# A perceiver block's delta rule: hand-laid order for TensorE and ScalarE, a quartered load of the coefficients, and a last round that also carries the MLP's gate weights and first u

## The chip, the cores and the metric

The kernel runs on one core of a Trainium2 chip. Its time is the device time of one launch, in microseconds (us), taken as the median of several runs. Before the change the median of 3 runs is 2965.88 us (2964.45 to 2977.48). All arithmetic of the parts told of here is in float32.

## What is computed

The input x has 128 sequences of 32 tokens and 512 features, 4096 tokens in all. Three layers follow each other, each with a layer norm ahead and its input added behind: a cross attention to a context, the layer shown here, and a feed-forward part with Hadamard rotations and ternary weights. The middle layer is the one that the change touches:

```python
h = _rms(x, attn_norm_w)
q = silu(silu(_causal_dwconv(h @ Wq.T, conv_q)))   # k and v likewise, with their weights
q = _l2norm(q.reshape(B, T, nh, hd))               # k likewise: each head divided by its length
beta = jax.nn.sigmoid(h @ Wbeta.T)
# for each token t in order, with a 16 x 16 state S for each of 32 heads:
#   err = S k_t - v_t;  S = S - beta_t * err k_t^T;  o_t = S q_t
o = _rms(o, out_norm_w) @ Wout.T
x = x + o
h2 = _rms(x, mlp_norm_w)
x = x + silu(h2 @ Wgate.T) * (h2 @ Wup.T) @ Wdown.T
```

The delta rule over 32 tokens is not run as a scan. Products k k^T and k q^T over the tokens of a sequence are formed first; a triangular substitution then gives a vector u for each token; and o is the masked product of k q^T with u, times 1/|q|.

## The kernel before, in words

The work stands in four stages, one after the other: cross attention (to about 690 us), the delta rule's products (`delta_products`, 696 to 1208 us), the delta rule's output with the MLP (`delta_out_mlp`, 16 blocks of 256 tokens, to about 2400 us), and the Hadamard feed-forward part.

**Rounds of the products.** `delta_products` goes through 8 groups of 512 tokens, a round each (`a_round`). A round has 12 channels of 128 features, four for each of q, k and v, in the order k0 q0 k1 q1 ... v0 v1 v2 v3. For one channel (`channels`), TensorE multiplies normed tokens hT by a slice of the weights into a PSUM bank pp (4 float32 matmuls of 128x512, L568; pp has three banks), ScalarE scales the bank into acc with the last tap of the convolution (L573), and VectorE adds the three other taps (L575). ScalarE then applies the silu twice (`activated`, L582 and L583). Between the channels a round also does this:

- `multiply` takes one *piece* (four heads' worth of products for 256 tokens, function `products`): 32 small matmuls into two banks pg (L495), a copy by ScalarE to kk (L501), a store of the coefficients to the DRAM tensor ld (L502), a masking by GpSimd (L506) and a store to pd (L507). One operand of a piece, kqm, is a copy of k and q laid out with zeros between, filled by eight small loads on SP's queue (`masked_operand`, L481). There are three kqm tiles, and hold fills one as soon as it is free. A round has eight pieces.
- `add` squares k and q on ScalarE (L619) and sums them per head, with beta's product, into the bank pn (L621 to L623). `lengths` takes the roots (tile f). `by_tokens` turns |k| and beta to tokens (L636), and inverts |k| squared and |q|. The latter is a maximum and a reciprocal on 32 partitions x 512 (L648, L649), stored to the DRAM tensor rq (L651).
- `put_v` turns v to tokens (L660), multiplies by |k| into vt (L663), adds beta as a last column (GpSimd, L667) and stores to vd (L669). It is done for the previous round's group in the first four channels of a round. For the last group it follows at the end, after `by_tokens`.
- `normed` prepares the next group's hT: a load, hn on VectorE (L559), four transposes and a copy.

**The substitution beside it.** `Substitution.solve` reads one group's coefficients (tile L, 2 MB, one load, L451 ff.) and vd (tile W). Its 32 steps are on VectorE: a short multiply (L458), a long product pr (L462) and a long subtraction (L468), whose length falls from 31 x 64 elements to 64. Steps are placed beside the rounds and, at a given pace, beside the MLP's blocks (`mixed` takes the next step of whichever list is least far along by its stated costs).

**Order on an engine.** The tile scheduler orders each engine's instructions by the program and its estimates; an engine executes its own list in order, and so does SP with its DMA issues. A class `InOrder` ties every instruction of an engine to the one before it. Before the change only the Hadamard stage uses it.

**The passage to the MLP.** The last round has the products of its own group left over: k and q go to a DRAM tensor kd (SP), and `late_products` does the eight pieces later, from kd, one per MLP block after the first ones. `delta_out_mlp` opens its own SBUF pools: weights wo (1 MB), wg and wu (2.8 MB each, loaded in two parts), wd (2.8 MB). It clears the operand tiles um, pe and km on GpSimd (L759). Then `back(0)` makes the first block's input: a load of u, GpSimd's copy into um (L791), 16 loads into pe per tile (L798), 32 matmuls (L805), oT (L818), a square, and the product with wo (L838), then y, its square, the root, and hT (L853). `load_rows` is L103. wg, wu are scaled by the norm's weights on ScalarE (L929), wo on VectorE. `mlp(b)` computes, for each of 11 slices, gate (L864) and up (L867), then silu and product, and at the end the down product (L875).

In the order of the SP queue before, wd follows `back(0)`'s first u load and stands before the second:

```python
load_rows(nc, wo, woT)
...
for cols in (slice(0, 6 * P), slice(6 * P, FF)):
    for t, src in ((wg, wgT), (wu, wuT)):
        load_rows(nc, t[:, :, cols], src[:, cols])
...
mixed((4.0, part(first, 4.0)), (1.0, part(late, 1.0)))
scaled_rows(nc, st, "onw", onorm_w, [wo])
load_rows(nc, wd, wdT)
```

Of the kernel before, what the change touches and what calls it, by code (L numbers as in the profile page):

```python
# [10 lines left out]
FP = mybir.dt.float32  # L11
# [46 lines left out]
class Ctx:  # L58
# [33 lines left out]
    def transposed(self, ps, x, ident, dtype=FP):  # L92

        rows, n = x.shape[0], x.shape[1] // P
        pt = ps.tile([P, n, rows], dtype, name="ps")
        for c in range(n):
            self.nc.tensor.transpose(pt[:, c, :], x[:, c * P : (c + 1) * P], ident[:rows, :rows])
        return pt


def load_rows(nc, dst, src):

    nc.sync.dma_start(dst, src.rearrange("(c p) n -> p c n", p=P))  # L103
# [15 lines left out]
def butterflies(nc, a, b):  # L119
# [9 lines left out]
    return a  # L129

# [304 lines left out]
class Substitution:  # L435
# [7 lines left out]
    def solve(self, gi):  # L443
        nc = self.nc
        L = self.pool.tile([P, T, H4, T], FP, name="L")
        nc.sync.dma_start(
            L.rearrange("p s h t -> p (s h t)"),
            self.ld[gi].rearrange("c (b s) f -> (c b) (s f)", s=T),
        )
# [7 lines left out]
        for s in range(T):  # L457
            nc.vector.tensor_mul(w[:, s], w[:, s], bc(W[:, s, :, HD], HD))  # L458
# [25 lines left out]
def products(nc, banks, pool, ld, pd, k, m, cm):  # L484
# [4 lines left out]
    for i in range(2):  # L489
        for r, pg in enumerate(pgs):  # L490
            rows = slice(r * P // 2, (r + 1) * P // 2)
            for j in range(4):
                js = slice(j * T, (j + 1) * T)
                ts = slice(i * P + j * T, i * P + (j + 1) * T)
                nc.tensor.matmul(  # L495
# [3 lines left out]
    for r, pg in enumerate(pgs):  # L499
        kk = pool.tile([P, 2, 2, H4, T], FP, name="kk")  # L500
        nc.scalar.copy(kk, pg)  # L501
# [8 lines left out]
        )  # L510


def delta_products(
# [11 lines left out]
    stack, (xp, wp1, hp, wk1, wp, st, wk, wp2, wk2, wp3, wk3, psn, psp, ps, psg) = pools(  # L525
        tc, ("b_x", 3), ("b_w1", 1), ("b_hn", 2), ("b_h", 2), ("b_w", 1), ("b_st", 2), ("b_k", 2),
        ("b_w2", 1), ("b_v", 2), ("b_m", 4), ("b_g", 6), ("b_pn", 1, PSUM), ("b_pp", 3, PSUM),
        ("b_ps", 2, PSUM), ("b_pg", 2, PSUM),
    )
    with stack:  # L530
        w, cw = {}, {}
        for n, src, p in (("k", wkT, wp1), ("q", wqT, wp1), ("v", wvT, wp2)):
            w[n] = p.tile([P, DC, D], FP, name=f"w{n}")
            load_rows(nc, w[n], src)
# [11 lines left out]
        kqm = [wp3.tile([P, H4, 2, KT], FP, name=f"kqm{i}", bufs=1) for i in range(3)]  # L546
# [8 lines left out]
        def normed(n, xt, hT):  # L555
# [6 lines left out]
            nc.scalar.copy(hT[:, :, i * P : (i + 1) * P], g.transposed(ps, hn, g.ident))  # L562

        def channels(hT, n, ec):

            pp = psp.tile([P, GB, T], FP, name="pp")
            for dc in range(DC):
                nc.tensor.matmul(  # L568
# [4 lines left out]
            nc.scalar.activation(acc, pp, AF.Copy, scale=cw[n][:, ec, TAPS - 1 : TAPS])  # L573
# [7 lines left out]
        def activated(acc, dst):  # L581
            nc.scalar.activation(acc, acc, AF.Silu)  # L582
            nc.scalar.activation(dst, acc, AF.Silu)  # L583
# [13 lines left out]
        def multiply():  # L597
# [3 lines left out]
                nc, lambda: psg.tile([P, 2, 2, H4, T], FP, name="pg"), wk3,  # L601
# [6 lines left out]
        class Group:  # L608
# [8 lines left out]
            def add(self, kq, hT, ec):  # L617
                sq = wk.tile([P, 2, SG], FP, name="sq")
                nc.scalar.activation(sq, kq, AF.Square)  # L619
                at = dict(start=ec == 0, stop=ec == DC - 1)  # L620
                nc.tensor.matmul(self.sums[0:H], hs[:, ec, :], sq[:, 0], **at)  # L621
                nc.tensor.matmul(self.sums[H : 2 * H], w["b"][:, ec, :], hT[:, ec, :], **at)
                nc.tensor.matmul(self.sums[2 * H :], hs[:, ec, :], sq[:, 1], **at)  # L623

            def lengths(self):

                f = self.factors = wk.tile([3 * H, SG], FP, name="f", bufs=1)
                nc.scalar.activation(f[H : 2 * H], self.sums[H : 2 * H], AF.Tanh, scale=0.5)
                for r in (slice(0, H), slice(2 * H, 3 * H)):
                    nc.scalar.activation(f[r], self.sums[r], AF.Sqrt)  # L630

            def by_tokens(self):
                f = self.factors
                pt = ps.tile([P, GT, 2 * H], FP, name="ps")
                for i in range(GT):
                    nc.tensor.transpose(  # L636
# [10 lines left out]
                q = f[2 * H :]  # L647
                nc.vector.tensor_scalar_max(q, q, 1e-12)  # L648
                nc.vector.reciprocal(q, q)  # L649
                for c in range(DC):  # L650
                    nc.gpsimd.dma_start(  # L651
                        rq[self.gi, :, :, c].rearrange("i h t -> h i t"),
                        f[2 * H + c * HH : 2 * H + (c + 1) * HH].rearrange("h (i t) -> h i t", t=P),
                    )

            def put_v(self, ec):
                v2 = self.v.pop(ec)
                pv = ps.tile([P, GT, P], FP, name="ps")
                for i in range(GT):
                    nc.tensor.transpose(pv[:, i, :], v2[:, i * P : (i + 1) * P], g.ident)  # L660
# [6 lines left out]
                nc.gpsimd.tensor_copy(vt[:, :, :, HD], self.beta[:, :, h])  # L667
# [5 lines left out]


# [3 lines left out]
        loads = (3, 4, 5, 9)  # L678

        def a_round(gi, old, hT, made):  # L680
# [3 lines left out]
            if gi + 1 < NG:  # L684
                hT_next = wk1.tile([P, DC, SG], FP, name="hT")
                made.append(hT_next)
            for j, (n, ec) in enumerate(todo):
                if n == "v":
                    dst = new.v[ec] = wk2.tile([P, SG], FP, name="v2", bufs=4)
                else:  # L690
                    if n == "k":
                        kq[ec] = wp3.tile([P, 2, SG], FP, name="kq")
# [5 lines left out]

                if due[j] and count["done"] < len(held) and (old or j >= 4):
                    multiply()  # L700
                activated(acc, dst)
                if n == "q":
                    if gi < NG - 1:
                        pieces.extend((gi, ec, half, kq[ec]) for half in range(SG // KT))
                        hold()
                    else:
                        nc.sync.dma_start(kd[:, ec], kq[ec])
                if 3 <= j <= 9 and j % 2:
                    new.add(kq[(j - 3) // 2], hT, (j - 3) // 2)
                if j in loads and gi + 1 < NG:  # L710
                    xt.append(load((gi + 1) * GT + len(xt)))
                if j == 9:
                    new.lengths()
                    if gi == 0:
                        g.factors(*(t[:, EARLY:] for t in stats))
                if j == 11:
                    new.by_tokens()
                if j >= 8 and gi + 1 < NG:
# [678 lines left out]
```

## Time and profile before

| | us |
|---|---|
| median of 3 runs | 2965.88 (2964.45 to 2977.48) |
| the profiled execution | 2972.53 |
| its span | 2970.8 |
| TensorE busy in the span | 2844.7 (96%) |
| VectorE busy | 2006.6 (68%) |
| ScalarE busy | 1042.0 (35%) |
| GpSimd busy | 672.3 (23%) |
| first product of the rounds (k of round 0) | 695.7 |
| starts of rounds 1 to 7 | 756.4, 816.2, 886.0, 956.2, 1019.0, 1088.7, 1156.0 |
| last product of the rounds ends | 1208.2 |
| first gate product of the MLP | 1264.3 |

The profile is of one execution. Its engines are PE (TensorE matmuls), PEld (TensorE's weight loads), DVE (VectorE), ACT (ScalarE), POOL (GpSimd) and SP (DMA issues). A busy time is the time in which an engine executes; L12 is a line of the kernel. The row "PEclk" shows the clock that TensorE was granted, in tenths of full speed. A chain of waits follows the work that ended last back from step to step, each to what released it. Rows of groups give busy time and the mean duration of one in ns, then the idle time ahead of them and what ended it. ScalarE's and VectorE's shares say little here, since the stages differ in what binds them; busy times by stage are more use.

### The profile page before, as it was taken

The numbers are of one execution on the slowest core, as the hardware profiler recorded it, in microseconds if no ns is written. First come the engines' busy times: TensorE is split into PE (matmuls) and PEld (weight loads), VectorE is DVE, ScalarE is ACT, GpSimd is POOL, SyncE is SP. The second block draws the span as 40 slices with busy tenths as digits, with TensorE's granted clock in tenths as the row PEclk, the third lists the DMA queues.
The fourth block names the chain that finished last, engine by engine and source line by source line (L and its number), as shares of the span: only waits on it lengthen the run. The fifth ranks groups of instructions, "written<-read, shape, count | busy, mean of one in ns | idle before, by whom it ended". The sixth has DMA issues, their size and how long they took to land.

```text
span 2970.8 us, 42807 instructions
## 1 busy us (share of the span) xinstructions
PE 2844.7 (96%) x15895; PEld 1667.3 (56%) x15958; DVE 2006.6 (68%) x3309; ACT 1042.0 (35%) x1772; POOL 672.3 (23%) x962
## 2 busy tenths in 40 slices
PE   8999999999999999599999999999999999999997
PEld 3444344443433433266767677777777756666664
DVE  3343444325699897368787878787722289999995
ACT  1111111114655656521211111111221146676774
POOL 1121212212676776321211110101010000000000
PEclk9999999999999999799999999999999999999998
DMA  9898998883554644741414131313131024444333
GB/s 316 278 308 281 329 315 282 278 276 103 169 151 125 183 129 120 222 149 56 136 53 131 50 123 51 116 44 106 65 119 47 20 71 87 89 80 89 86 71 67
DMA packets 337951, 428.59 MB, mean 144 GB/s; under 512 B 149072, under 2 KB 248528, under 8 KB 334288
## 3 DMA queue, kind: packets, MB, share of 16 engines
q1 hardware_dynamic: 301664, 325.93, 36.3%
q0 software_dynamic: 36080, 99.92, 11.2%
q8 instruction: 127, 2.08, 0.3%
q14 instruction: 80, 0.66, 0.1%
HBM read 288.36 MB, written 93.85 MB: 129 GB/s over the span
## 4 chain that ended last, share of the span: by engine, by line
PE 57%; DVE 11%; DMA 3%; issue 2%; ACT 1%; POOL 1%; SPq 0%; DVEq 0%; ACTq 0%; POOLq 0%
PE ps L950 18%; PE pm L864 9%; PE pm L875 9%; PE pm L867 9%; PE pp L568 4%; PE ps L838 4%; DVE W L468 3%; DVE acc L575 3%; DVE pr L462 2%; PE ps L805 2%; PE pg L495 1%; DMA xs<-x 1%; DMA wd<-in_WdownT_dram 1%; POOL kk L506 0%; DVE f L649 0%
## 5 line engine op out<-in xcount | busy, mean ns | idle before, releaser
L864 PE MATMUL pm<-hT,wg 128*128 128x256 f32 x1408 | 342.4, 386 | 0.9 <-ACT hT L853 0.9
L867 PE MATMUL pm<-hT,wu 128*128 128x256 f32 x1408 | 336.2, 382 | 0.0
L462 DVE TENSOR_TENSOR pr<-L,W 128x1984 f32<-128x1984 f32 (+30 forms) x248 | 308.9, 1245 | 31.5 <-DMA L<-ld 27.3
L468 DVE TENSOR_TENSOR W<-W,pr 128x1984 f32<-128x1984 f32 (+30 forms) x248 | 312.4, 1260 | 3.1
L875 PE MATMUL pm<-wd,mT 128*128 128x512 f32 x704 | 307.4, 592 | 0.0
L864 PEld LDWEIGHTS pm<-hT,wg 128*128 128x128 f32 x1408 | 263.5, 191 | 50.6 <-issue 12.1
L867 PEld LDWEIGHTS pm<-hT,wu 128*128 128x128 f32 x1408 | 269.3, 192 | 36.8 <-ACT kk L501 0.3
L875 PEld LDWEIGHTS pm<-wd,mT 128*128 128x128 f32 x704 | 132.6, 190 | 160.1 <-issue 159.1
L950 PE MATMUL ps<-wq,qT 128*128 128x512 bf16 x930 | 217.2, 381 | 4.5 <-ACT t L950 3.0
L869 ACT ACTIVATE sg<-pm 128x256 f32<-128x256 f32 x176 | 66.8, 381 | 325.5 <-PE pm L864 315.4
L870 DVE TENSOR_TENSOR mT<-pm,sg 128x256 f32<-128x256 f32 x176 | 73.8, 419 | 154.4 <-PE pm L867 143.8
L950 DVE TENSOR_TENSOR mb<-m 128x1024 f32<-128x1024 f32 x128 | 153.3, 1218 | 0.1
L950 PEld LDWEIGHTS <-qT 128*128 128x128 bf16 x960 | 94.3, 98 | 105.0 <-issue 6.1
L950 DVE TENSOR_TENSOR m<-mb 128x1024 f32<-128x1024 f32 x128 | 150.8, 1220 | 1.2
L1178 POOL DMA_DIRECT2D xo<-x x31 | 26.4, 851 | 530.8 <-ACT xo L950 480.3
L950 ACT ACTIVATE t<-ps,magic,qs 128x512 f32<-128x512 f32 x158 | 115.6, 780 | 34.4 <-DVE qs L950 34.4
L568 PE MATMUL pp<-hT,wk 128*128 128x512 f32 x256 | 125.5, 634 | 0.7 <-ACT hT L562 0.7
L950 PEld LDWEIGHTS ps<-hd,mT 128*128 128x128 f32 x1024 | 120.8, 194 | 8.9 <-ACT mT L950 4.8
L950 PE MATMUL ps<-hd,mT 128*128 128x128 f32 x1024 | 121.4, 278 | 4.0 <-ACT mT L950 4.0
L950 PE MATMUL ps<-wq,q2T 128*128 128x512 bf16 x481 | 119.3, 392 | 5.5 <-DMA q2T<-q 3.8
L502 POOL DMA_DIRECT2D ld<-kk x128 | 93.3, 729 | 129.1 <-ACT kk L501 120.5
L506 POOL TENSOR_TENSOR kk<-kk,cm 128x256 f32<-128x256 f32 x128 | 121.0, 945 | 2.5
(225 smaller groups left out, 4808.8 us busy)
## 6 DMA issues: line engine op xcount, KB each, us to landing
kall<-in_ctxT_dram SPq DMA_DIRECT2D x32, 2056.0 KB
cx<-in_ctx_dram SPq DMA_DIRECT2D x32, 2048.0 KB
x<-xo POOLq DMA_DIRECT2D x64, 256.0 KB, 3.4
ld<-kk POOLq DMA_DIRECT2D x128, 128.0 KB, 2.6
pd<-kk POOLq DMA_DIRECT2D x128, 128.0 KB, 2.6
L<-ld SPq DMA_DIRECT2D x8, 2048.0 KB
pe<-pd SPq DMA_DIRECT2D x256, 64.0 KB
kqm<-kq SPq DMA_DIRECT2D x448, 32.0 KB
```

The costliest lines, as they stand in the source:

```text
L462: nc.vector.tensor_mul(pr[:, 0:n], bc(L[:, s, :, s + 1 : T].rearrange("p h t -> p t h"), HD), w[:, s].unsqueeze(1).to_broadcast([P, n, H4, ...
L468: nc.vector.tensor_sub(w[:, s + 1 :], w[:, s + 1 :], pr[:, 0:n])
L502: nc.gpsimd.dma_start(ld[r].rearrange("(i p) f -> p i f", p=P), kk[:, 0].rearrange("p i h t -> p i (h t)"))
L506: nc.gpsimd.tensor_mul(q, q, cm.unsqueeze(1).to_broadcast([P, 2 * H4, T]))
L568: nc.tensor.matmul(pp.rearrange("p b t -> p (b t)"), w[n][:, dc, ec * P : (ec + 1) * P], hT[:, dc, :], start=dc == 0, stop=dc == DC - 1,)
L575: last = nc.vector.scalar_tensor_tensor(acc[:, :, d:], pp[:, :, : T - d], cw[n][:, ec, TAPS - 1 - d : TAPS - d], acc[:, :, d:], ALU.mult, ...
L838: nc.tensor.matmul(pw, oT[:, i, dc, :], wo[:, dc, :], start=dc == 0, stop=dc == DC - 1)
L864: nc.tensor.matmul(pg, wg[:, dc, fs], hT[:, dc, :], start=dc == 0, stop=dc == DC - 1)
L867: nc.tensor.matmul(pu, wu[:, dc, fs], hT[:, dc, :], start=dc == 0, stop=dc == DC - 1)
L870: mark[:] = [nc.vector.tensor_mul(mT[:, fc, :], pu, sg).ins]
L875: nc.tensor.matmul(pd, mT[:, fc, i * P : (i + 1) * P], wd[:, fc, :], start=fc == 0, stop=fc == FC - 1,)
L950: ins = method(*args, **kw).ins
```

## The change

It has these parts.

- **Order.** `InOrder` moves up in the file and gets a helper `follow`. In the rounds, all of TensorE's and ScalarE's instructions go through it, so they run in the order in which the program names them. The silus of a channel are called one channel later (`waiting`); `square` and `add` are apart; `by_tokens`, `put_q` and `put_v` of a group lie in channels 1 to 5 of the next round (`behind_round`).
- **1/|q|.** The roots are stored to rq as they are. Later (`inverted`) they are loaded back as a 128x128 tile, rl, limited and inverted on VectorE, and stored. The load is on SP, the stores are on POOL. For the last group this happens in the MLP.
- **Coefficients.** `solve` loads L in four quarters of 8 rows, each called for 8 steps ahead.
- **Pools.** The SBUF pools of both stages are laid out anew, so that those of wo, wg and `back`'s small tiles take the place of tiles that the rounds are done with early. um, pe and the u tiles are made ahead of the rounds, on the other side of SBUF, and cleared there.
- **Last round.** `last_round` takes its channels in the order k0 to k3, v0 to v3, q0 to q3; the sums, roots and `by_tokens` for k and beta come before q, and the first two `put_v` lie inside the round. The stores of kd move from SP to POOL. wo and wg are loaded, wo is scaled on VectorE and wg on ScalarE, and the first u and its matmuls are tied to places ahead of the round's last channels.
- **After it.** wu follows the round's last stores of vd and kd, then causal and wd. wu is scaled on VectorE. `late_products` starts with one piece in block 1 and does one per block to block 9; the last group's 1/|q| is inverted in block 10.

In the order of instructions of the changed kernel, the number of solve steps (pr) in rounds 1 to 6 is 3, 9, 18, 10, 9, 0, where before it is 2, 8, 12, 10, 8, 9.

The core of the diff:

```diff
+def follow(tc, ins, other):
+    tc.add_manual_dep(
+        ins, other.name,
+        mybir.DependencyInfo(mybir.DependencyClass.NoSync, mybir.DependencyReason.DATA),
+        reason="in order",
+    )
...
-        nc.sync.dma_start(
-            L.rearrange("p s h t -> p (s h t)"),
-            self.ld[gi].rearrange("c (b s) f -> (c b) (s f)", s=T),
-        )
+        rows = self.ld[gi].rearrange("c (b s) f -> (c b) s f", s=T)
+        some = T // 4
+        def load(s):
+            nc.sync.dma_start(
+                L[:, s : s + some].rearrange("p s h t -> p s (h t)"), rows[:, s : s + some]
+            )
+        load(0)
...
         for s in range(T):
+            if s % some == 0 and s + some < T:
+                load(s + some)
...
+def inverted(nc, rq, r):
+    every = rq.rearrange("i h c t -> (i h c) t")
+    nc.sync.dma_start(r, every)
+    yield
+    nc.vector.tensor_scalar_max(r, r, 1e-12)
+    nc.vector.reciprocal(r, r)
+    nc.gpsimd.dma_start(every, r)
+    yield
...
+    pe = InOrder(tc, nc.tensor)
+    act = InOrder(tc, nc.scalar)
...
-                q = f[2 * H :]
-                nc.vector.tensor_scalar_max(q, q, 1e-12)
-                nc.vector.reciprocal(q, q)
...
+            if j == 1:
+                old.by_tokens()
+                old.put_q()
+                old.inverse = inverted(
+                    nc, rq[old.gi], st.tile([P, P], FP, name="rl", bufs=1)
+                )
+            if 2 <= j <= DC + 1:
+                old.put_v(j - 2)
+            if j in (8, 10):
+                next(old.inverse)
...
+            for j, (n, ec) in enumerate((n, ec) for n in "kvq" for ec in range(DC)):
...
+        weights = load_rows(nc, wo, woT)
+        with tc.issue_after(weights.ins):
...
+            first = back(0)
+            next(first)
+            for i in left["q"]:
+                follow(tc, i, last["pe"].ins)
...
+            for i in left["pool"]:
+                follow(tc, i, last["pool"].ins)
+            weights = loaded(wg, wgT)
+        scaled(nc.scalar.mul, wg)
+        with tc.issue_after(weights.ins):
...
+            for engine in ("pe", "act"):
+                for i in left[engine]:
+                    follow(tc, i, last[engine].ins)
+            loaded(wu, wuT)
+            nc.sync.dma_start(cm, causal)
+            weights = load_rows(nc, wd, wdT)
+        scaled(nc.vector.tensor_scalar_mul, wu)
```

## The prediction, on record before the changed kernel ran

> **What bounds the kernel now.** I read the 40 slices of the page first, then the busy times stage by stage, then the chain that ended last around the one slice that stands out.
>
> ```profile
> PE   8999999999999999599999999999999999999997
> DVE  3343444325699897368787878787722289999995
> PEclk9999999999999999799999999999999999999998
> ```
>
> TensorE is busy everywhere but in slice 17 (1188 to 1262 us), where it falls to 5 and its granted clock to 7. That is the passage from the delta rule's rounds to the MLP. The second view cuts this part of the span by stage: rounds 1 to 6 of the products, then the passage, then the first full stretch of the MLP. Columns: length, busy time and count for PE, PEld, DVE, ACT and POOL, then the granted clock, DMA share and GB/s.
>
> ```profile
> 756.40:816.20 59.80, 59.13 (x403) 25.36 (x402) 35.77 (x49) 39.08 (x63) 42.66 (x61) 1.00 0.60 182
> 816.20:886.00 69.80, 63.36 (x423) 26.83 (x423) 69.60 (x82) 41.29 (x67) 53.83 (x71) 0.96 0.55 148
> 886.00:956.20 70.20, 65.11 (x413) 27.55 (x413) 67.74 (x89) 40.17 (x66) 48.91 (x65) 0.91 0.48 132
> 956.20:1019.00 62.80, 61.65 (x413) 26.25 (x412) 49.58 (x83) 39.74 (x65) 43.39 (x63) 0.98 0.57 162
> 1019.00:1088.70 69.70, 63.09 (x417) 26.28 (x415) 67.06 (x78) 40.87 (x67) 52.40 (x66) 1.00 0.57 163
> 1088.70:1156.00 67.30, 64.15 (x411) 27.12 (x410) 64.18 (x76) 39.66 (x65) 47.69 (x64) 0.98 0.43 114
> 1208.20:1272.00 63.80, 31.75 (x352) 18.94 (x352) 22.89 (x41) 27.61 (x42) 24.51 (x37) 0.71 0.76 222
> 1272.00:1343.00 71.00, 71.00 (x416) 49.96 (x409) 49.35 (x88) 14.46 (x27) 15.10 (x20) 1.00 0.47 142
> ```
>
> The MLP's blocks are TensorE alone (71.00 of 71.00). The rounds are bound in turn by VectorE (816: 69.60 of 69.80) and by TensorE (756: 59.13 of 59.80). The passage is bound by neither. Its chain says by what:
>
> ```profile
> 1210.46 13.15 DMA u<-ud
> ...
> 1224.47 16.95 DMA wd<-in_WdownT_dram
> ...
> 1248.19 1.93 PE ps L805 x32
> ```
>
> The first u comes 13 us late, behind the gate and up weights on the one SP queue; the second u is issued only after the 2.8 MB of wd have landed. TensorE's gate matmul (L864) starts at 1264.3, 56.1 us after the last product of the rounds (1208.2).
>
> **The change, part by part.** Sums are against the profiled execution, 2972.5 us (span 2970.8 and 1.7 around it), 6.7 above the median of 2965.9.
>
> *The passage.* The last round computes all k, then v, then q, so n, beta and half of put_v lie inside it. wo and wg get room that is free before the round ends, so wo, wg and the 8 scalings of wg (ScalarE, 0.87 us each) and the first u with its 32 matmuls (L805) go into the round. ScalarE has 52.2-30.8 = 21 us free there, and 8 x 0.87 = 7 us fit. Left after the last q channel, at E:
> - acc 3 x 0.71, two silus 0.63 each, put_v transposes, and the kd store of q's last quarter. That store is issued on POOL, and the order of the changed kernel lets wu's load (SP) wait for it. My count is E+10: scale 0.7, acc 2.1, silus 1.3, store issue 0.7, a landing of 5 for 0.5 MB.
> - wu's first half is 1.5 MB. Before, one such load took 6.5 us (issued 1208.9, landed 1215.4): E+16. Its scaling is on VectorE now, 4 x 0.7 for the first half (the 128x512 scaling of wo took 0.48; 768 columns give 0.72): E+19.
> - Beside that: second u's 32 matmuls (1 to 2 us), sqrt and ro, wo's matmuls, y, square, hT. In the chain of before this ran from 1248.2 to 1263.6, 15.4 us, with wd's wait taken out: gate at E+16, up at E+19.
>
> So the MLP runs from E+19 in place of E+56.4: -37.4. Against this: two late products that ran in the passage now run inside TensorE-bound blocks, 2 x 1.03 = +2.1; the second block's pe loads stand behind wd on SP and come about when they are needed, 0 to 3, +1; the last round gains the first tile's 32 matmuls, +1. km's clearing and late k loads: nothing waits, the pieces start a block later.
>
> A rule weighs against this sum. Windows of 8 us show the clock at 0.50 from 1220 to 1252 and then restored:
>
> ```profile
> 1236.00:1244.00 8.00, 3.12 (x46) 1.95 (x40) 2.81 (x7) 0.63 (x1) 0.00 (x0) 0.50 0.71 202
> 1244.00:1252.00 8.00, 5.08 (x50) 2.00 (x38) 0.54 (x1) 1.17 (x2) 2.93 (x5) 0.50 0.64 194
> 1252.00:1260.00 8.00, 8.00 (x73) 3.99 (x79) 2.72 (x6) 2.90 (x5) 3.47 (x4) 0.99 0.43 118
> ```
>
> The Trainium skill (TensorE: Matmul & The Clock Gate, "What's actually happening") says that an idle window of some 3.4 us halves the clock and one busy window restores it. Before, TensorE was warm when the gate matmuls began, since 8.0 us of work stood in front. In the changed kernel E+6 to E+16 is nearly idle, so the first gate matmuls run cold: by the rule 1.7 us lost; by the row 1244 to 1252, a stretch of 5.1 us busy that stayed at 0.50 throughout, 2.5. I take +2. The passage then gives -37.4+2.1+1+1+2 = -31.3. Unknown: kd's landing (2.6 as for a 128 KB store, or 7 as for vd here) shifts it by -2 to +3; with wd's cover gone it may be +5.
>
> A second rule speaks against moving stores to POOL: the skill (SBUF — State Buffer, "SBUF: two separate sides") lets VectorE and GpSimd exclude each other on a shared port and lets a GpSimd-issued DMA wait for it, 3.1 us in place of 0.6. The rows agree for GpSimd's arithmetic and not for its issues. First 756 to 816, then 1019 to 1089, where VectorE solves:
>
> ```profile
> L506 POOL TENSOR_TENSOR kk<-kk,cm 128x256 f32<-128x256 f32 x15 | 12.4, 824 | 0.3
> L507 POOL DMA_DIRECT2D pd<-kk x15 | 11.1, 739 | 1.5 <-POOL kk L506 1.5
> ```
>
> ```profile
> L506 POOL TENSOR_TENSOR kk<-kk,cm 128x256 f32<-128x256 f32 x16 | 19.8, 1239 | 0.3
> L507 POOL DMA_DIRECT2D pd<-kk x17 | 12.4, 731 | 3.0 <-POOL kk L506 3.0
> ```
>
> The multiply goes from 0.82 to 1.24 us, the issue stays at 0.73. By the rule the kd store costs 2.5 us on the path, by the row nothing. The last round has no solve steps; I take the row.
>
> *The rounds.* 1/|q| was a maximum and a reciprocal on 32 partitions x 512 (0.42 and 3.34 us, L648 and L649). As 128x128, loaded back from DRAM, the reciprocal takes 0.94, which is what that of n takes (L645, the same shape), and the maximum 0.3, estimated from its 0.42. That frees 2.5 us of VectorE per round. TensorE in hand order removes its waits for ScalarE's kk and sq in the rounds (13.5+5.7 us in all; not additive to VectorE's bound). The sum over rounds 1 to 6 of the larger of PE and DVE is 59.1+69.6+67.7+61.7+67.1+64.2 = 389.4, the time 399.6; so 10 us are stalls and 389 is imbalance, for VectorE in all has 353.9 and TensorE 376.5. In the order of the changed kernel the solve steps of these rounds are 3, 9, 18, 10, 9 and 0 (before 2, 8, 12, 10, 8, 9). A step with n rows left is two operations on 64n elements a partition (2.28 and 2.18 us at 1984) and a short one of some 0.4; at 1.05 to 1.15 ns an element I take 1.05, since the larger overshoots the sum of the rounds before. The other work of VectorE is 35 us a round (36 conv sums of 0.71, hn 4 x 0.65, vt 4 x 0.68, and the factors). That makes VectorE 48, 67, 67, 71.5, 60, 35, in all 348 where 353.9-6 x 2.5 = 339 would do, so rather too much. With a TensorE floor of 60 (round 1's 59.8): 60+67+67+71.5+60+60 = 385.5. I add half of the old stalls, 5.5: 391, so -9. Bounds: 376.5 (perfect balance, -23) and 415 (+15, third rival). Round 0 has six products in place of seven, -1, given to later rounds where VectorE hides it.
>
> *L in four transfers.* VectorE waited 27.3 us for L, of which 2.0 in the rounds; the other 25.2 lie in MLP blocks that TensorE binds. A first quarter that lands sooner is worth at most the 2.0; if a later quarter is late, a step waits some us, in the same cover. I take -1.
>
> Sum: -31.3-9-1-1 = -42.3. Profiled 2930; on the median 2965.9-42.3 = 2923.6, say 2924.
>
> **The rivals.**
> 1. Only the passage pays (0.21). VectorE's order is as uneven as before, and rounds and L give nothing: 2965.9-31.3 = 2935. For it: 71.5 in one round; against: the freed 2.5 us per round.
> 2. The rounds balance as well (0.13): hand order spreads TensorE's slack, 376.5 plus 5 of stalls: -18 in place of -9, and 2915; with perfect balance 2910.
> 3. Slower (0.07): 1/|q|'s round trip. Four rq stores on POOL (0.57 each, landing 3.5 to 5.2), a load (2.0 to 2.6, as pe), and then VectorE's maximum, which stands in order just after the new round's first or second channel. By count the data are there 11 to 15 us into a round and VectorE asks at 10 to 15: 0 to 4 us, times 7 rounds. While VectorE waits, the conv sums behind it wait, three pp banks fill, and TensorE, which may no longer pick another piece, stops; SP holds the kqm loads behind the rl load. It decides from 42/7 = 6 us a round; at 8 us, 7 x 8 = 56, less 42: +14, 2980. Against it: 399.6 us hold only 10 of stalls and VectorE lags in its heavy rounds, so it asks late.
> 4. No change (0.08): the same at 4 to 6 us a round or wu and wd not earlier than E+35, 2951 to 2966.
>
> **How the numbers follow.** The sum as it stands has 0.51, around 2924 (2915 to 2932 with the passage's -2 to +5 and the rounds' halves). A measurement tells 0.5%, 14.8 us, from no change, so faster is below 2951: cases 0.51+0.21+0.13 = 0.85. Same 0.08, slower 0.07. The range reaches from full balance with an early wu, 2900, to the edge of the fourth case, 2952.
>
> **What would show it.** Right: slice 17 at 7 or more; gate matmul 17 to 22 us after the last pp product; the waits of ps on um (15.8 us) and the 17 us chain step of wd gone; a 2 us cold start; rounds 1 to 6 in about 391 us, VectorE at 67 to 71 in three of them. Wrong: VectorE or SP waiting on rl for over 2 us a round; wu landing later than E+18; TensorE waiting in the rounds for a product's operand because it may not pass it; blocks 1 to 9 of the MLP longer than 71.5 us.

## The result and the profile after

The changed kernel takes 2939.44 us in the median of 4 runs (2935.05 to 2941.03), the kernel before 2967.86 (4 runs). The ratio is 0.9897, with a 95% interval of 0.987 to 0.9923: 28 us less, where the prediction said 42 (2924). The profiled execution took 2938.77 us and its span is 2937.0, 33.8 less than before; the profiled execution of before was 4.7 us above its median, so the two profiles differ by more than the medians do. Line numbers below are those of the changed file; instructions that go through InOrder all have line L151.

A ledger of the two spans, each boundary read from a timeline, tells where the 33.8 went. xo is the output tile of the cross attention, so "last xo" is its last addition on VectorE. The joint is what lies between that and the rounds' first product, the passage what lies between their last product and the MLP's first gate product.

| stretch | before, us | after, us | difference |
|---|---|---|---|
| cross attention, to its last xo | 691.55 | 687.31 | -4.2 |
| joint: last xo to first k product | 4.14 | 14.84 | +10.7 |
| round 0 | 60.70 | 58.63 | -2.1 |
| rounds 1 to 6 | 399.86 | 393.68 | -6.2 |
| last round | 51.95 | 55.86 | +3.9 |
| passage: last product to first gate product | 56.06 | 19.70 | -36.4 |
| MLP, first gate to last down product | 1128.6 | 1134.6 | +6.0 |
| Hadamard part | 577.9 | 572.4 | -5.5 |

The first and the last row are not counted as the change's: the changed kernel and the ten variants below share the code of both, and their last xo lies between 681.3 and 693.1 us, their Hadamard part between 572.3 and 576.5 (577.9 before, in one execution). The six rows between come to -24.1.

The page's slices, after:

```profile
PE   8999999997999899999999999999999989999997
DVE  3353544325599995678787878888722289999996
PEclk9999999999999999999999999999999999999999
```

The 5 in TensorE's row and the 7 in the clock's have gone. A new 7 stands in the tenth slice (661 to 734 us), where no step of the prediction looked. By stage (round 2, round 4, the passage to the first up product, the MLP's first 71 us):

```profile
821.27:885.91 64.64, 61.10 (x417) 26.20 (x413) 64.54 (x78) 40.40 (x66) 54.33 (x66) 1.00 0.56 155
951.88:1030.06 78.18, 65.92 (x416) 27.62 (x412) 72.03 (x98) 40.61 (x65) 55.10 (x67) 0.89 0.55 166
1210.32:1236.00 25.68, 21.36 (x181) 11.94 (x180) 11.47 (x24) 13.04 (x23) 11.57 (x16) 0.93 0.96 280
1236.00:1307.00 71.00, 71.00 (x366) 49.96 (x369) 50.85 (x94) 13.05 (x24) 9.68 (x10) 1.00 0.52 163
```

From the last product to the first up product TensorE idles 4.3 us of 25.7, where before it idled 32 of 57.9. Round 4 is the exception among the rounds: 78.18 us with neither engine full. The chain through the passage no longer holds a load of u or wd; the part of it from the first gate product on:

```profile
1230.09 2.68 PE pm L1009 x8
1232.77 1.69 PE ps L953 x54
...
1234.49 0.06 DVE oT L963
...
1235.09 0.62 DVE wu L1070
...
1235.76 0.70 PE pm L1012 x2
```

With E for the end of the rounds' last product (1210.32), the first gate product (L1009) is at E+19.7. The first up product (L1012) is at E+25.4: it waits for wu's scaling, which in VectorE's order stands behind the second tile's oT, and this behind the products with um (L953).

### The profile page after: what moved, and what is told of

It reads as the page before. It is cut to its first block, busy times and chain, and to the rows that moved or that the text cites. A ratio compares the mean times of both kernels' runs of the same rounds, so it can differ in the third digit from the quotient of the medians.

```text
span 2937.0 us, 42773 instructions
## 1 busy us (share of the span) xinstructions
PE 2823.2 (96%) x15895; PEld 1658.6 (56%) x15958; DVE 1995.4 (68%) x3317; ACT 1033.0 (35%) x1766; POOL 682.5 (23%) x974
## 4 chain that ended last, share of the span: by engine, by line
PE 59%; DVE 10%; issue 2%; DMA 2%; POOL 1%; ACT 1%; SPq 1%; ACTq 0%; DVEq 0%; POOLq 0%
PE ps L151 18%; PE pm L1009 9%; PE pm L1020 9%; PE pm L1012 9%; PE pp L151 5%; PE ps L983 4%; DVE W L503 2%; DVE pr L497 2%; DVE acc L625 2%; PE ps L953 2%; PE pg L151 1%; PE pn L151 1%; DMA xs<-x 1%; POOL kk L541 1%; DVE m L151 1%
## 5 line engine op out<-in xcount | busy, mean ns | idle before, releaser
L1009 PE MATMUL pm<-hT,wg 128*128 128x256 f32 x1408 | 343.1, 386 | 0.2 <-ACT hT L998 0.2
L1012 PE MATMUL pm<-hT,wu 128*128 128x256 f32 x1408 | 336.8, 382 | 1.3 <-DVE wu L1070 1.3
L1009 PEld LDWEIGHTS pm<-hT,wg 128*128 128x128 f32 x1408 | 263.9, 191 | 51.0 <-issue 11.5
L1012 PEld LDWEIGHTS pm<-hT,wu 128*128 128x128 f32 x1408 | 268.7, 191 | 38.7 <-DVE wu L1070 1.6
L151 PE MATMUL ps<-wq,qT 128*128 128x512 bf16 x930 | 215.5, 379 | 6.2 <-ACT t L151 4.6
L151 PEld LDWEIGHTS <-qT 128*128 128x128 bf16 x960 | 94.0, 98 | 105.3 <-issue 5.5
L151 DVE TENSOR_TENSOR mb<-m 128x1024 f32<-128x1024 f32 x128 | 153.2, 1217 | 0.1
L151 DVE TENSOR_TENSOR m<-mb 128x1024 f32<-128x1024 f32 x128 | 150.8, 1219 | 1.2
L151 ACT ACTIVATE t<-ps,magic,qs 128x512 f32<-128x512 f32 x158 | 115.7, 781 | 39.5 <-DVE qs L151 39.4
L151 PEld LDWEIGHTS ps<-hd,mT 128*128 128x128 f32 x1024 | 119.1, 192 | 8.9 <-ACT mT L151 4.8
L151 PE MATMUL ps<-hd,mT 128*128 128x128 f32 x1024 | 119.8, 275 | 4.0 <-ACT mT L151 4.0
L151 PE MATMUL ps<-wq,q2T 128*128 128x512 bf16 x481 | 116.2, 384 | 5.4 <-DMA q2T<-q 3.7
L151 PE MATMUL pp<-hT,wk 128*128 128x512 f32 x256 | 120.3, 614 | 0.7 <-ACT hT L151 0.7
```

Of the source, the lines that this page charges most:

```text
L151: got = method(*args, **kw)
L1009: nc.tensor.matmul(pg, wg[:, dc, fs], hT[:, dc, :], start=dc == 0, stop=dc == DC - 1)
L1012: nc.tensor.matmul(pu, wu[:, dc, fs], hT[:, dc, :], start=dc == 0, stop=dc == DC - 1)
```

## Experiments

Each is the changed kernel with the edit shown (its core; `...` marks what is left out). The runs came in groups, each with the kernel before in it: its median is 2967.86 us beside the changed kernel, 2973.45 beside e_clear, e_clear_hn, e_wlate and e_free, 2968.49 beside e_all, e_kdsp, e_wgafter and e_rqold, 2972.31 beside e_wlate_free and e_wlate_oneL. So medians of two groups can be up to 5.6 us apart for no reason of the edit, and the runs of one kernel spread by 0.1 to 0.7%. Ratios are to the kernel before of the same group.

Stage lengths of the profiles are the sharper measure, but not all to the same degree. The joint is 14.8 to 14.9 us in the eight kernels that share it. Rounds 1 to 6 take 392.0 to 395.1 in the five that share them, the MLP 1132.3 to 1138.9 in the eight whose blocks are the same. So a difference of under 3 us in those rounds, or under 7 in the MLP, says nothing.

### The joint: clearing and scaling

The timeline around 690 us (start, length, engine, line, operation), first of the kernel before, then of the changed one. Only VectorE's scalings, xo and hn, GpSimd's clearings and the first product k are shown:

```profile
683.20 0.46 DVE L432 TENSOR_SCALAR wk<-wk,nw 128x512 f32<-128x512 f32 x1
...
687.08 0.66 DVE L432 TENSOR_SCALAR wb<-wb,nw 128x32 f32<-128x32 f32 x4
...
691.55 0.69 DVE L336 TENSOR_TENSOR xo<-ps,xt 128x512 f32<-128x512 f32 x1 [3.80 <-PE ps L332]
...
695.69 2.06 PE L568 MATMUL pp<-hT,wk 128*128 128x512 f32 x2
```

```profile
687.31 0.69 DVE L364 TENSOR_TENSOR xo<-ps,xt 128x512 f32<-128x512 f32 x1 [5.18 <-PE ps L360]
687.92 0.48 DVE L460 TENSOR_SCALAR wk<-wk,nw 128x512 f32<-128x512 f32 x1
688.83 1.86 POOL L1476 MEMSET um<- 128x1024 f32 x2
688.92 3.80 DVE L460 TENSOR_SCALAR wk<-wk,nw 128x512 f32<-128x512 f32 x1
690.61 1.82 POOL L1476 MEMSET pe<- 128x2048 f32 x1
692.73 2.47 DVE L460 TENSOR_SCALAR wk<-wk,nw 128x512 f32<-128x512 f32 x2
692.86 2.06 POOL L1476 MEMSET pe<- 128x2048 f32 x1 [0.42 <-DVE mv L82]
...
698.86 0.99 DVE L609 TENSOR_SCALAR hn<-xt,mv,rs 128x512 f32<-128x512 f32 x2
...
702.15 1.22 PE L151 MATMUL pp<-hT,wk 128*128 128x512 f32 x1 [0.68 <-ACT hT L151]
```

A scaling of 128x512 takes 0.48 us when alone. The one that starts 0.1 us after GpSimd's first clearing has begun takes 3.80 and ends 0.3 us after the third clearing; the next two take 2.47 beside the fourth. After that VectorE goes on to scale wq, wv and wb before it gives hn, for which TensorE waits 11.4 us. Before the change the clearings of um and pe stood in the last round (1182 to 1196 us), and all 12 scalings of wk, wq and wb were done ahead of the cross attention's last xo, at 683 to 688 us. In the changed kernel they stand behind it, though VectorE idled for 5.2 us just before xo. wk's load is issued 32 us later than before (658.5 and 626.3), but still 29 us ahead of the first scaling; whether it is what changed the scheduler's order, no run shows.

**e_clear.**

```diff
-        for t in (*um, *pe):
-            nc.gpsimd.memset(t, 0.0)
...
                     multiply()
+                    if clears:
+                        one = nc.gpsimd.memset(clears.pop(0), 0.0)
+                        follow(tc, one.ins, stored_last[-1])
```

> The changed kernel with one move: the four clearings of um and pe on GpSimd (5.7 us) leave the start of the products, where they lie beside VectorE's scaling of the weights, and stand behind the first four pieces of round 0. Theory A (GpSimd's clearing locks VectorE out: the second scaling of wk took 3.80 us in place of 0.47 and the next two 2.47 in place of 0.93): the first k product, which stood at 702.2 us, comes 4.9 us sooner, at about 697.3, the four scalings of wk take 0.5 us each, and the time is about 2934. Rival B (the start is late only because all scalings stand ahead of hn in VectorE's order): the first k product stays at 702, time 2939.

Measured: joint 9.89 us in place of 14.84, so 4.95 less, as theory A has it, with the scalings of wk back at their own length:

```profile
685.66 0.48 DVE L460 TENSOR_SCALAR wk<-wk,nw 128x512 f32<-128x512 f32 x1
...
686.66 0.47 DVE L460 TENSOR_SCALAR wk<-wk,nw 128x512 f32<-128x512 f32 x1
687.14 0.85 DVE L460 TENSOR_SCALAR wk<-wk,nw 128x512 f32<-128x512 f32 x2
```

The first k product was at 694.95, lower than expected because this execution's cross attention ended 2.3 us sooner. The time, 2937.91 (2937.08 to 2939.49), hardly shows it: its profile has 1.9 us more in the rounds, 2.2 more in the MLP and 3.6 more in the Hadamard part. The ratio is 0.9881 where the changed kernel's is 0.9897, which would be 4.7 us, but their intervals overlap. The stage shows theory A, the time alone would not.

**e_clear_hn.**

```diff
-        scaled_rows(nc, wp, "nw", norm_w, [w["k"], w["q"], w["v"], w["b"]])
+        nw = scaled_rows(nc, wp, "nw", norm_w, [w["k"]])
...
             normed(i, load(i), hT)
+        for t in (w["q"], w["b"], w["v"]):
+            for dc in range(DC):
+                nc.vector.tensor_scalar_mul(t[:, dc, :], t[:, dc, :], nw[:, dc : dc + 1])
```

> As the former, and in addition the scalings of wq, wb and wv stand behind the remaining two hn of the first group. Theory A with order as a second share: those 12 scalings are 4.0 us (1.66 + 1.66 + 0.67), so the first k product comes at about 693.5 and the time is about 2930. If only the clearing matters: as the former, 697. If only the order matters: about 698 here too and 702 in the former.

Measured: joint 5.3 us (last xo 681.88, first k product 687.20), another 4.6 less, and a time of 2929.45 (2922.45 to 2935.41; ratio 0.9851). So of the 10.7 us lost in the joint, 5 are the lock-out by the clearing and nearly 5 the order of the scalings; 1.2 are left.

### Round 4: a load that holds SP's queue

SP's issues in the changed kernel:

```profile
967.87 1.42 SPq L478 DMA_DIRECT2D L<-ld  x2
977.12 0.32 SPq L484 DMA_DIRECT2D W<-vd  x1
977.55 4.86 SPq L516 DMA_DIRECT2D kqm<-kq  x7
```

and TensorE's wait in round 4 (us in total, times, longest):

```profile
PE pg L151 <- DMA kqm<-kq: 8.4, 2, 7.7
```

W's load is for the third solve, which is due in the MLP. Its buffer is the first solve's, and is free only when the result of that (ud) has been stored. That store was issued at 967.3 and took 9.8 us to land, at 977.1, and SP waited for it with round 4's operand copies behind:

```profile
SPq L484 <- DMA ud<-W: 7.7, 1, 7.7
```

**e_wlate.**

```diff
-        nc.sync.dma_start(
+        got = nc.sync.dma_start(
             W.rearrange("p t h v -> p (t h v)"),
...
+        if gi:
+            follow(self.tc, got.ins, self.step)
...
-                nc.vector.tensor_sub(w[:, s + 1 :], w[:, s + 1 :], pr[:, 0:n])
+                last = nc.vector.tensor_sub(w[:, s + 1 :], w[:, s + 1 :], pr[:, 0:n])
+                if s == 24:
+                    self.step = last.ins
```

> The changed kernel with one move: W's load of the next solve may not stand in SP's queue before step 24 of the solve before it. In round 4 it stood ahead of the kqm loads, waited for the store of the former W, and let go of the queue only at 977.1; TensorE then waited 8.4 us for kqm in hand order. Theory C (that wait is the 78.2 us of round 4): no wait of TensorE for kqm above 1 us, round 4 at 70 to 72 us, rounds 1 to 6 near 386 in place of 393.7, time about 2932. Rival D (round 4 is bound by VectorE's 72 us of work and the wait is only its shadow): the wait goes, round 4 stays within 3 us of 78, the time within 3 us of 2939.

Measured: round 4 at 68.6 us, rounds 1 to 6 at 381.5, time 2926.27 (2922.83 to 2931.87; ratio 0.9843). The wait, the row of round 4 and SP's queue at the same place:

```profile
PE pg L151 <- DMA kqm<-kq: 0.8, 1, 0.8
```

```profile
943.73:1012.29 68.56, 62.98 (x416) 27.03 (x412) 67.20 (x97) 40.68 (x67) 57.39 (x68) 0.95 0.62 188
```

```profile
957.56 0.79 SPq L479 DMA_DIRECT2D L<-ld  x2
958.53 0.32 SPq L557 DMA_DIRECT2D rl<-rq  x1
958.90 0.90 SPq L479 DMA_DIRECT2D L<-ld  x2
962.23 12.82 SPq L521 DMA_DIRECT2D kqm<-kq  x13
```

The kqm copies leave 18.5 us into round 4 in place of 25.7. Theory C holds, rival D falls. Round 4 gains 9.6 us and the six rounds 12.2, more than the wait of 8.4; VectorE's busy time in round 4 fell too, from 72.0 to 67.2. The larger of TensorE's and VectorE's busy time, round by round, now sums to 379.1 us against 381.5 of span: 2.4 us of stall are left in six rounds, where the changed kernel has 10.2.

**e_wlate_oneL** is e_wlate with L in one load again:

```diff
-        some = T // 4
+        some = T
```

> The changed kernel with W's load moved behind step 24, and with L in one load of 2 MB again. If the quarters are worth only the first wait: VectorE waits for L some 1 to 3 us more in the rounds, and some 20 us more in the MLP's blocks, where TensorE binds; time within 3 us of 2926. If a late first step in the MLP holds back the u of a block: the MLP is longer by 5 us or more, time 2931 or above.

Measured: 2951.70 (2948.14 to 2954.87), 25 us more than e_wlate, and neither expectation as it was meant: the time is above 2931, but not by the MLP. There VectorE waits 25.0 us for L at no cost that shows: 1136.8 us against 1136.1. The loss that is the edit's is in the rounds: 397.9 against 381.5. (The span is 29 us longer; 11.8 of that is a cross attention that ended later in this execution.) Of these 16.4 us round 4 alone has 9.0 (77.6 against 68.6). SP's queue says why:

```profile
972.64 0.32 SPq L557 DMA_DIRECT2D rl<-rq  x1
981.05 0.32 SPq L479 DMA_DIRECT2D L<-ld  x1
981.47 55.23 SPq L521 DMA_DIRECT2D kqm<-kq  x64
```

The one load waits 8.0 us until the solve before it has read its last row (by its product pr), and holds all kqm copies behind it until 981; TensorE waits 7.9 us for kqm in this round. It is W's fault at another load. The other 7.4 us are spread over rounds 2, 3 and 5 (2.2 to 3.5 each), where the scheduler's order of the solve steps differs, and their cause stays open, as does what the quarters are worth in the changed kernel itself.

### What the hand order is worth

**e_free** leaves rounds 0 to 6 to the scheduler; **e_wlate_free** does so with W's load moved. Their edit:

```diff
-            if self.last is not None:
+            if self.last is not None and self.strict:
                 follow(self.tc, got.ins, self.last)
...
+        pe.strict = act.strict = False
         for gi in range(NG - 1):
...
+        pe.strict = act.strict = True
         mixed((len(todo), last_round(NG - 1, old, hT)), *beside(NG - 1))
```

> The changed kernel with rounds 0 to 6 not in hand order (the scheduler orders TensorE and ScalarE there, as before the change); the last round and all else as changed. If the hand order brings the rounds' gain: rounds 1 to 6 back near 400 us, time about 2945. If the gain is from the reciprocal that VectorE no longer does (2.5 us a round): rounds 1 to 6 stay near 390 to 394 and the time near 2939. If the hand order costs (TensorE waits behind a piece whose operand is late): below 390, time about 2933.

> The changed kernel with W's load moved behind step 24 (rounds 1 to 6 then took 381.5 us, the time was 2926), and in addition rounds 0 to 6 not in hand order. With W out of the way the share of the hand order itself can be read: if it spreads the work, rounds 1 to 6 go back by more than 6 us, to 388 to 396, time about 2936. If the scheduler's order is as good once no wait of SP holds a strict order up: within 3 us of 381.5, time within 4 us of 2926.

Measured: e_free has 397.7 us in rounds 1 to 6 and 2950.43 us (2940.64 to 2961.17); e_wlate_free has 396.4 and 2945.36 (2940.78 to 2950.63). Against their strict twins, 393.7 and 381.5, hand order is worth 4.0 us with W's load in the way, little more than the rounds vary by, and 14.9 with it moved. Read the other way, moving W gains 12.2 us in hand order and 1.3 in the scheduler's, which fits that a late operand costs most where TensorE may not take something else first. In e_free the wait for kqm is 3.3 us in place of 8.4. Of the 14.9, 6.2 are a better spread (the larger busy time of each round sums to 385.3 us in e_wlate_free and 379.1 in e_wlate), and 8.7 are fewer stalls.

### The reciprocal

**e_rqold** computes 1/|q| as before the change, for the last group too, and drops the inversion in the MLP:

```diff
             def put_q(self):
+                q = self.factors[2 * H :]
+                nc.vector.tensor_scalar_max(q, q, 1e-12)
+                nc.vector.reciprocal(q, q)
...
-                old.inverse = inverted(
-                    nc, rq[old.gi], st.tile([P, P], FP, name="rl", bufs=1)
-                )
```

> The changed kernel with 1/|q| computed as before the change: maximum and reciprocal on 32 partitions x 512 (0.42 and 3.34 us), no loading back, no tile rl. If the shorter reciprocal frees VectorE in the rounds that it binds: rounds 2 to 5 are longer by 2.5 us each, rounds 1 to 6 about 404 in place of 393.7, time about 2949. If the trip through DRAM costs what it saves (waits, or the place in the order): rounds 1 to 6 within 3 us of 393.7, time within 3 us of 2939.

Measured: rounds 1 to 6 in 396.8 us, time 2952.11 (2944.74 to 2960.53; ratio 0.9936). Neither expectation fits: the rounds are only 3.1 us longer than in the changed kernel, no more than they vary by, but the time is 12.7 longer. VectorE's busy time in the six rounds is 355.7 us against 337.4, 3.0 a round; 2.6 of that are the longer maximum and reciprocal (0.42 and 3.34 us in place of 0.23 and 0.94), so the change does free VectorE. What that is worth in the rounds can't be told, since the order changed with the edit: round 4 has 53.4 us of VectorE in place of 72.0, TensorE waits for kqm only 2.3 us, and the larger busy time of each round sums to 381.9 us, less than the changed kernel's 383.5.

Where it does show is the passage. There the last group's 1/|q| now stands in the chain (its reciprocal, then its store, then xs behind the store on GpSimd):

```profile
1228.53 3.36 DVE f L717
...
1232.16 1.48 POOL rq L720 x3
...
1234.38 1.28 POOL xs L986
...
1235.68 1.48 DVE y L994
```

The gate product is at E+24.6 in place of E+19.7 and up at E+31.1 in place of E+25.4. So 4.9 us of the passage's gain hang on putting off the last group's 1/|q| to the MLP, an item that the prediction didn't count. The MLP is 7.6 us longer here; why is open.

### The passage

**e_wgafter** loads wg behind wu:

```diff
-            weights = loaded(wg, wgT)
-        scaled(nc.scalar.mul, wg)
...
+            for cols in parts:
+                up_part = load_rows(nc, wu[:, :, cols], wuT[:, cols])
+                gate_part = load_rows(nc, wg[:, :, cols], wgT[:, cols])
+                follow(tc, gate_part.ins, up_part.ins)
...
+        scaled(nc.scalar.mul, wg)
```

> The changed kernel with wg's two loads not in the last round but behind wu's, part by part (wu, wg, wu, wg, wd). If the early gate weights are what shortens the passage: the first gate product waits for 1.5 MB more, some 5 us beyond wu's landing, and for four scalings; it comes at about E+29 in place of E+19.7, up with it (E+25.5 now), so the passage is 4 to 6 us longer and the time about 2944. If the first u and wo in the last round are the larger part and wu binds anyway: up within 1 us of E+25.5 and the time at 2939.

Measured: gate at E+28.4, up at E+32.0, time 2945.06 (2941.02 to 2951.91; ratio 0.9923). The first expectation holds for the gate and the time, and up is 3 us later than it said. wg in the round is worth 8.7 us to the gate product, 6.5 to up and 5.6 in the medians. The larger part of the passage's gain, from E+56 to E+28, is there without it. The chain of before, with 13.2 us for the first u and 17.0 for wd, says where that comes from: the first u in the round, wo, and wd no longer ahead of the second u. No run takes these apart.

**e_kdsp** stores kd from SP:

```diff
-                return lambda: left["pool"].append(nc.gpsimd.dma_start(kd[:, ec], kq[ec]).ins)
+                return lambda: nc.sync.dma_start(kd[:, ec], kq[ec])
```

> The changed kernel with kd's four stores on SP instead of POOL. In the changed kernel they took 5.5 to 9.5 us to land, and wu's load was issued 16.3 us after the last k, v or q product, when the last of them had landed. Theory E (a store from GpSimd's queue is slow in itself): on SP they land in 3 to 5 us, wu is issued at E+11 to E+12, the first up product comes at about E+20.5 in place of E+25.5, time 2 to 4 us less. Rival F (the DMA engines are full there with pe, xs, vd and r): they land in 5 to 9 us from SP too, or stand behind SP's pe loads; wu at E+16, time within 2 us.

Measured: wu is issued at E+14.4 in place of E+16.3, 8.8 us after the last kd store; time 2935.35 (2933.84 to 2948.8; ratio 0.9898, the changed kernel's 0.9897). Mostly rival F: in the changed kernel the DMA engines are 0.92 to 1.04 busy from E on, and wu waits for vd's stores too (3.8 us, and 1.1 for kd), which took up to 9.9 us. Up comes at E+24.2, but so it does in e_clear_hn and e_wlate_free, whose kd stores are on GpSimd and whose wu left at E+14.9 and E+16.4. Within these 2 us the departure of wu's load does not set when up comes; the chain, with oT ahead of wu's scaling, agrees.

### All three moves

**e_all** joins e_clear_hn and e_wlate.

> The changed kernel with the three moves together: clearing of um and pe behind the first pieces, 12 of the 16 weight scalings behind hn, W's load behind step 24 of the solve before. If the parts are independent, as their stages lie apart: the step from the last xo of the cross attention to the first k product 7.2 us (14.8 in the changed kernel), rounds 1 to 6 in 381.5 us (393.7), 19.8 less in all, so about 2919. If the earlier start only moves a wait into the rounds (operands or loads that come at their own time): less than 12 of it shows, 2927.

Measured: 2923.07 (2915.0 to 2923.94), ratio to the kernel before 0.984 (0.9821 to 0.9859): below both the kernel before and the changed one. Joint 5.3 us, rounds 1 to 6 383.4, together 19.8 less than the changed kernel in the stages, as the first expectation has it, and 16 in the medians, between the two. The parts add up in their stages. In the times this is not shown: e_wlate alone has a ratio of 0.9843, and its runs overlap with these.

## Why the prediction was right and where it was not

It foresaw the direction, and for the passage the mechanism; its size was 42 us, and 28 were measured. In the stages that the change touches the profiles differ by 24.1 us: 4.8 are missing in the passage, 2.7 in the rounds with L, and 10.7 were lost in the joint, which the prediction left out. The number itself is nearest to the first rival (only the passage pays, 2935), but not for its reason: the rounds did pay, and the joint took it back.

- **The passage, -31.3.** Measured: -36.4 to the gate product, +3.9 in the last round, +6.0 in the MLP (no more than that varies by), together -26.5. The step was right in kind, but its sum has a slip: the -37.4 sets the new up product (E+19) against E+56.4 for the old gate, which stood at E+56.1, while up stood at E+57.9. Up against up it should say -38.9, and -32.5 were measured. Mis-sized was the way to up. kd's landing was taken as 5 us and was 9.5, so wu left at E+16.3 in place of E+10; and wu's scaling stood behind the second tile's oT. Up came at E+25.4. The gate product was bound by the chain through wo, y and hT, at E+19.7 in place of E+16. The last round grew by 3.9 and not 1; TensorE's busy time in it grew by 3.2 (51.9 to 55.1), since half of put_v moved in beside the matmuls of u: work moved, not lost. Counted from the first up product the MLP is 2.0 us longer, which would be the two late products (2.1).
- **The cold clock, +2.** The rule gave 1.7 us, the row 2.5; measured are 1.7, but not for the reason given. The prediction took TensorE for nearly idle from E+6 to E+16; to E+14 it was busy, with sums, um and wo. It idled for 2.98 us only, just ahead of the transposes of y at 1227.61, and then the clock was low for two windows of 2 us in which TensorE never stopped:

```profile
1228.00:1230.00 2.00, 2.00 (x17) 1.25 (x15) 1.09 (x2) 1.44 (x3) 0.00 (x0) 0.54 0.85 258
1230.00:1232.00 2.00, 2.00 (x7) 1.67 (x7) 0.00 (x0) 1.02 (x1) 0.00 (x0) 0.60 1.02 413
```

  At 0.54 and 0.60 that is 0.92 + 0.80 = 1.7 us. That the 2 came out is luck in part.
- **The rounds, -10.** Measured -8.3 with round 0, but not as worked out. The sum of the larger engine was put at 385.5 plus 5.5 of stalls. In the changed kernel it is 383.5 plus 10.2, since a new wait, W's load, ate most of what was saved; in e_wlate it is 379.1 plus 2.4. VectorE's busy time, 337.4 us (335.1 in e_wlate), was near the 339 that the text found by subtraction and not its 348. Nor is 376.5 the bound for perfect balance: TensorE's own busy time fell to 366.8 us in e_wlate. Why is open; part of it may be the clock, which was 0.91 in one round of before and at least 0.95 in all of e_wlate.
- **Rival 3** was of the right kind, at the wrong load. SP does hold kqm copies while TensorE may not pass them, but behind W, in one round, for 8.4 us. This was one of the text's own signs of being wrong. rl kept VectorE waiting 1.7 us in rounds 1 to 6 and 2.2 in the last one.
- **L, -1.** The wait in the MLP was free, as the text had it (e_wlate_oneL: 25.0 us of it, and the MLP no longer). But the text looked at the wait for L alone, and not at what the L load keeps waiting behind it on SP.
- **What it left out: the joint.** The change moves the clearing of um and pe from the last round, where nothing waited for it, to the start of the products, and with the new pools the scalings of the weights fall behind the last xo. The prediction gave neither a cost: +10.7. It even named the rule that applies (the Trainium skill, SBUF — State Buffer, "SBUF: two separate sides": of a GpSimd instruction and a VectorE instruction that needs the port they share, the one that starts first keeps it for the whole instruction). It asked it only of kd's stores, where no run shows it (the page's 3.1 us are for a store beside a VectorE copy, while the rows set against it have the solve's products and subtractions). It did not ask it of the clearings, where it is worth 5 us: 3.80 us for a scaling of 0.48. With the joint and W put right, e_all comes to 2923.1. That this is the 2924 of the forecast is chance: these steps are not those that the forecast had summed.

## What to carry to other kernels

Every instruction that a change moves has to be costed at its new neighbours, clearings too: here a GpSimd clearing that was free in one stage locked VectorE out in another. When an engine is put in strict order, look at each queue that feeds it for a load whose buffer is freed late. Such a load delays all that stands behind it in the queue, so it should be placed no earlier than the instruction that frees its buffer. And an item put off from a passage is worth what it would take on the passage's chain, not its share of an engine's busy time.

## What the runs showed of the hardware

- A VectorE scaling of 128x512 float32 in SBUF (0.48 us) took 3.80 us when it started 0.1 us after a GpSimd clearing had begun (changed kernel), and 0.47 with the clearings gone (e_clear). It was held through three clearings in a row.
- kd's stores of 0.5 MB each, from GpSimd's queue, took 5.5 us to land while the DMA engines were 0.80 and 0.87 busy, 8.1 and 9.5 while they were full (1.05 and 0.99; changed kernel).
- After 2.98 us without a product TensorE's clock was 0.54 and 0.60 in the following windows of 2 us, at a cost of 1.7 us (changed kernel).
- One load on SP whose buffer was not yet free held SP's queue for 7.7 us (W, changed kernel) and 8.0 us (L, e_wlate_oneL), with all operand copies behind it.
- Executions of nearly the same program differ by up to 12 us in where the cross attention ends and by 4 in the Hadamard part. A gain of 5 us is read from its stage, not from a median of four.
